# A perceiver layer's cross attention: the values' bias laid into PSUM by ACT, and outputs accumulated by ACT and POOL

## The chip, the cores and the metric

The kernel runs on one core of one Trainium2 chip. A core has a matrix engine (PE, with its weight loads shown apart as PEld), a vector engine (DVE), an activation engine (ACT), a general engine (POOL) and a queue that starts transfers (SP). Matrix products land in PSUM, a small memory of eight banks; DVE and ACT read and write PSUM, POOL here works on SBUF alone. The metric is device time in microseconds; each engine works through its own queue in order, and engines wait for each other by semaphores.

## The reference, cut to what matters

A layer of a perceiver in float32: cross attention of 128 queries per batch over a context of 2048 rows, then self attention, then a gated attention block. Batch 4, width 512, 16 heads of 32. The change lies in the cross attention alone:

```python
q = (layernorm(x) @ Wq + bq).reshape(4, 128, 16, 32)
k = (ctx @ Wk + bk).reshape(4, 2048, 16, 32)
v = (ctx @ Wv + bv).reshape(4, 2048, 16, 32)
scores = einsum('bqhd,bkhd->hbqk', q, k) / sqrt(32)
attn = softmax(scores over the 64 pairs of head and batch)   # not over the keys
out = einsum('hbqk,bkhd->bqhd', attn, v)
x = x + out @ Wo + bo
```

The softmax runs over the 64 (head, batch) pairs at one (key, query) position. So a block of keys can be finished by itself: no maximum or sum is carried from block to block, and the outputs of the blocks are simply added.

## The kernel before, in words

The context is cut into 16 blocks `n` of 128 keys (`NK` = 16, all four batches in one tile `ct`), and each block's heads into four chunks `c` of four heads. One pass of the inner loop over (`n`, `c`), called a step here, works on several blocks at once, in an order written out by hand (`manual_schedule`: every engine gets its instructions in the order of the program text). In a step of the steady part:

- `keys`: PE projects the next chunk of keys into a PSUM bank (L232), ACT copies it out with its bias (`kT`, L282).
- `values(n-1, c)`: PE projects the values of block `n-1` for batch `c` into a bank (L239), ACT copies them to `v` (L288), and POOL adds the bias row `bv_row` to `v` (L289).
- `shifted`, `exponentials_of`, `total` for block `n-1`: DVE subtracts the maximum (L342), ACT takes exponentials (L351), POOL adds up the sums (L355 to L358, and L331, L333 at the block's end).
- `attend(*done)`: PE multiplies the finished weights `sg` of block `n-2` and `v` into the bank `pso` (L386). `done` is the chunk that was scaled one step earlier.
- `scores(n, c)`: PE makes the scores in four banks (L299); ACT copies them to `sg` in two halves (L312).
- `scaled(n-2, c)`: DVE multiplies by the inverse sums (L342 again, the same helper).
- `accumulate(*done)`: DVE adds `pso` onto `acc` in SBUF (L399; for block 0 it copies, L397).
- `largest(n, c)`: DVE takes the maximum over the four banks of scores (L321, and L319 at `c` = 0); at the next block's start `largest_tail` folds it (L336).

The pools set who waits for whom: keys and values share two banks in turn (`s12_ps`, 2 buffers), the scores have four, and `pso` is a single bank (`s1_ps_o`, 1 buffer), so an `attend` waits until the one before has been read out of it. The pool `tmp` has four tiles of 128x512 under the tag `xn`.

After the loop comes a written-out ending. It attends the last scaled chunk (13, 3), shifts and exponentiates block 15, projects the rest of its values, starts the output projection with an identity product (L519), adds up the last sums on PE in `ps_sum` (L525, whose last part waits for POOL's `half_total`, L366), and then alternates `scaled`, `attend`, `accumulate` and the output projection (L546).

## Time and profile before

| | |
|---|---|
| Time, median of 3 runs | 832.28 us (831.68 to 833.19) |
| Profiled execution, its own time | 832.41 us |
| Profiled execution, span | 830.6 us |
| Granted PE clock, mean | 0.999 |
| PE busy | 813.8 us (98%) |
| DVE busy | 629.7 us (76%) |
| ACT busy | 424.4 us (51%) |
| POOL busy | 438.1 us (53%) |
| Cross attention loop and its ending | to about 644 us of the span |

Busy times are sums over one execution; L with a number is a line of the kernel. In the timeline each row is: start in us, length in us, engine, line, operation, output<-inputs, sizes, how many instructions are merged (x), and in brackets how long the engine had been idle just before and what released it. Ends of matrix products are modelled, so their starts are the firmer number.

### The profile page before, as it was taken

How to read it: one execution, taken by the hardware profiler on the slowest of the kernel's cores; microseconds unless marked ns; L12 is line 12 of the kernel's file. 1: busy time of each engine (PE TensorE's matmuls, PEld its weight loads, DVE VectorE, ACT ScalarE, POOL GpSimd, SP SyncE). 2: the span in 40 equal slices, each digit the busy share in tenths (PEclk: the TensorE clock that was granted, in tenths of full speed). 3: DMA queues.
4: the chain of work that ended last, by engine and by line, in shares of the span. 5: the costliest groups of instructions: out<-in, count | busy, mean ns of one | idle time of the engine just before them, and what ended most of it. 6: DMA issues, size and time to landing. Idle time of an engine off the chain costs nothing. (4 is left out here: it accounts for less than half of the span.)

```text
span 830.6 us, 16415 instructions
## 1 busy us (share of the span) xinstructions
PE 813.8 (98%) x7089; PEld 442.7 (53%) x7089; DVE 629.7 (76%) x636; ACT 424.4 (51%) x689; POOL 438.1 (53%) x290
## 2 busy tenths in 40 slices
PE   9999999999999999999999999999989999999998
PEld 5444455555555555555545555555544558684574
DVE  2139689889888988988898898979896488947472
ACT  2357555555555555455545654555440435934661
POOL 1244776765666576666667575666760004512251
PEclk9999999999999999999999999999999999999999
DMA  8140010101101010101101010100110132102001
GB/s 313 31 155 1 1 52 2 51 1 51 36 17 52 1 52 1 51 8 47 51 1 52 1 51 2 52 2 6 48 51 1 51 102 105 36 18 86 19 1 52
DMA packets 11418, 35.54 MB, mean 43 GB/s; under 512 B 1121, under 2 KB 1522, under 8 KB 9298
## 3 DMA queue, kind: packets, MB, share of 16 engines
q1 hardware_dynamic: 9122, 30.36, 10.6%
q10 hardware_dynamic: 1776, 3.28, 1.1%
q8 instruction: 55, 0.90, 0.4%
q0 software_dynamic: 448, 0.87, 0.4%
q14 instruction: 17, 0.14, 0.1%
HBM read 33.45 MB, written 1.05 MB: 42 GB/s over the span
## 5 line engine op out<-in xcount | busy, mean ns | idle before, releaser
L342 DVE TENSOR_TENSOR sg<-sg,stat 128x2048 f32<-128x2048 f32 x128 | 288.2, 2281 | 1.2
L239 PE MATMUL ps_v<-w_xattn_Wv,ct 128*128 128x512 f32 x512 | 230.1, 593 | 0.0
L232 PE MATMUL ps_k<-ct,w_xattn_Wk 128*128 128x512 f32 x480 | 221.9, 605 | 0.8 <-ACT pos L142 0.8
L321 DVE TENSOR_TENSOR mx<-mx,ps_s 128x1024 f32<-128x1024 f32 x96 | 117.2, 1221 | 75.7 <-ACT sg L312 63.5
L239 PEld LDWEIGHTS ps_v<-w_xattn_Wv,ct 128*128 128x128 f32 x512 | 96.9, 190 | 121.4 <-issue 117.8
L289 POOL TENSOR_TENSOR v<-v,row_xattn_bv 128x512 f32<-128x512 f32 x64 | 81.7, 1277 | 144.9 <-ACT v L288 144.9
L351 ACT ACTIVATE sg<-sg 128x2048 f32<-128x2048 f32 x64 | 122.5, 1914 | 32.0 <-DVE sg L342 32.0
L232 PEld LDWEIGHTS ps_k<-ct,w_xattn_Wk 128*128 128x128 f32 x480 | 86.2, 189 | 94.1 <-issue 86.1
L357 POOL TENSOR_TENSOR sm<-sm,sg 128x1024 f32<-128x1024 f32 x46 | 108.5, 2359 | 35.9 <-ACT sg L351 33.7
L312 ACT COPY sg<-ps_s 128x1024 f32<-128x1024 f32 x128 | 123.4, 1013 | 7.2 <-DVE mx L319 3.5
L288 ACT COPY v<-ps_v 128x512 f32<-128x512 f32 x64 | 37.6, 587 | 157.3 <-PE ps_v L239 157.3
L358 POOL TENSOR_TENSOR sm<-sm,sg 128x1024 f32<-128x1024 f32 x46 | 108.8, 2365 | 3.6
L282 ACT ACTIVATE kT<-ps_k,bk 128x512 f32<-128x512 f32 x64 | 43.9, 689 | 66.3 <-PE ps_k L232 60.4
L299 PE MATMUL ps_s<-qT,kT 32*128 32x128 f32 x2048 | 75.7, 283 | 0.1
L386 PEld LDWEIGHTS pso<-sg,v 128*32 128x32 f32 x1920 | 48.8, 109 | 46.0 <-DVE sg L342 20.9
L299 PEld LDWEIGHTS ps_s<-qT,kT 32*128 32x128 f32 x2048 | 63.3, 186 | 18.0 <-issue 17.0
L386 PE MATMUL pso<-sg,v 128*32 128x128 f32 x1920 | 64.6, 276 | 2.2 <-DVE sg L342 1.6
L355 POOL TENSOR_TENSOR sm<-sg 128x1024 f32<-128x1024 f32 x16 | 37.9, 2370 | 37.3 <-ACT sg L351 37.3
L680 POOL TENSOR_TENSOR lg<-lg,pos 128x512 f32<-128x512 f32 x6 | 7.4, 1291 | 72.9 <-ACT lg L679 72.9
L399 DVE TENSOR_TENSOR acc<-pso,acc 128x512 f32<-128x512 f32 x54 | 36.9, 683 | 3.9 <-PE pso L386 3.9
L319 DVE TENSOR_TENSOR mx<-sg,ps_s 128x1024 f32<-128x1024 f32 x16 | 19.4, 1212 | 22.8 <-ACT sg L312 22.8
L1049 POOL TENSOR_TENSOR e<-e,rs 128x512 f32<-128x512 f32 x16 | 16.3, 1041 | 36.8 <-DVE rs L1048 36.8
(224 smaller groups left out, 821.4 us busy)
## 6 DMA issues: line engine op xcount, KB each, us to landing
ct<-in_ctxT SPq DMA_DIRECT2D x15, 1024.0 KB, 5.0
ev_win<-in_tabv SPq DMA_DIRECT2D x1, 2048.0 KB, 7.2
w_xattn_Wk<-in_xattn_Wk ACTq DMA_DIRECT2D x4, 256.0 KB, 7.9
ct<-in_ctxT SPq DMA_DIRECT2D x4, 256.0 KB, 6.4
x<-in_x SPq DMA_DIRECT2D x4, 256.0 KB, 7.7
w_xattn_Wv<-in_xattn_Wv ACTq DMA_DIRECT2D x1, 1024.0 KB
w_xattn_Wq<-in_xattn_Wq SPq DMA_DIRECT2D x1, 1024.0 KB, 10.1
w_xattn_Wo<-in_xattn_Wo ACTq DMA_DIRECT2D x1, 1024.0 KB, 5.0
```

The costliest lines, as they stand in the source:

```text
L232: nc.tensor.matmul(ps, lhsT=w[:, k, c * P : (c + 1) * P], rhs=src[:, k, :], start=(k == 0), stop=(k == C - 1))
L239: nc.tensor.matmul(ps, lhsT=src[:, k, b * T : (b + 1) * T], rhs=w[:, k, :], start=(k == 0), stop=(k == C - 1))
L282: nc.scalar.activation(kT[n, c], ps, AF.Identity, bias=bk[:, c : c + 1])
L289: nc.gpsimd.tensor_tensor(v[n, b], v[n, b], bv_row, ALU.add)
L299: nc.tensor.matmul(ps[i][:, cols], lhsT=kT[n, c][rows, cols], rhs=qT[rows, c, cols], start=True, stop=True)
L312: nc.scalar.copy(sg[n, c][:, k * HALF : (k + 1) * HALF], pss[n, c][k])
L321: nc.vector.tensor_tensor(mxs[n], mxs[n], pss[n, c][k], ALU.max)
L342: nc.vector.tensor_tensor(g, g, stat[:, row, :].unsqueeze(1).to_broadcast([P, NH * B, T]), op)
L351: nc.scalar.activation(sg[n, c], sg[n, c], AF.Exp, scale=SCALE)
L357: eng.tensor_tensor(t, t, g[:, 0:HALF], ALU.add)
L358: eng.tensor_tensor(t, t, g[:, HALF:], ALU.add)
L386: nc.tensor.matmul(ps[i * HD : (i + 1) * HD, b * T : (b + 1) * T], lhsT=v[n, b][:, h * HD : (h + 1) * HD], rhs=sg[n, c][:, f * T : (f + 1) ...
```

## The change

Two parts, both in the cross attention.

The first: after the values (`n`, `b`) of blocks 1 to 14 are copied out of their bank, ACT copies `bv_row` from SBUF into the bank that the next values will use (`bias_first`), and those values' four products all add onto it (`start` is false for the first of them). The POOL addition to `v` is left out for these. The values of block 0, of block 15 and (1, 0) keep it. That is 55 of the 64.

The second: `accumulate` for block 0 is an ACT copy instead of a DVE copy. For blocks 1 to 13, without the last chunk (13, 3), ACT copies `pso` to a tile `o` in SBUF and POOL adds `o` onto `acc`; that is 51 chunks. From (13, 3) on, DVE accumulates as before.

```diff
+        def bias_first(n, b):
+            biased[n, b] = bank(f"v{n}_{b}")
+            nc.scalar.copy(biased[n, b], bv_row)
+
         def values(n, b):
             v[n, b] = vp.tile([P, D], F32, tag="v", name=f"v{n}_{b}")
-            ps = bank(f"v{n}_{b}")
-            project(ps, wv, cts[n], b)
+            ahead = (n, b) in biased
+            ps = biased[n, b] if ahead else bank(f"v{n}_{b}")
+            for k in range(C):
+                nc.tensor.matmul(
+                    ps,
+                    lhsT=cts[n][:, k, b * T : (b + 1) * T],
+                    rhs=wv[:, k, :],
+                    start=(k == 0 and not ahead),
+                    stop=(k == C - 1),
+                    skip_group_check=ahead,
+                )
             nc.scalar.copy(v[n, b], ps)
-            nc.gpsimd.tensor_tensor(v[n, b], v[n, b], bv_row, ALU.add)
+            if not ahead:
+                nc.gpsimd.tensor_tensor(v[n, b], v[n, b], bv_row, ALU.add)
+            if 0 < n < NK - 1 and (n, b) != (NK - 2, B - 1):
+                bias_first(*((n, b + 1) if b + 1 < B else (n + 1, 0)))
...
         def accumulate(n, c):
             if n == 0:
-                nc.vector.tensor_copy(acc[:, c, :], pso[n, c])
+                nc.scalar.copy(acc[:, c, :], pso[n, c])
+            elif n < NK - 2 and (n, c) != (NK - 3, C - 1):
+                o = tmp.tile([P, B * T], F32, tag="xn", name=f"o{n}_{c}")
+                nc.scalar.copy(o, pso[n, c])
+                nc.gpsimd.tensor_tensor(acc[:, c, :], o, acc[:, c, :], ALU.add)
             else:
                 nc.vector.tensor_tensor(acc[:, c, :], pso[n, c], acc[:, c, :], ALU.add)
```

In the order that the program text gives, an ACT step becomes: `kT` copy, `v` copy, bias copy, exponential, two score copies, `o` copy. In the changed kernel's numbering the bias copy is L289, the `v` copy L304, the `o` copy L420 (block 0: L417), POOL's addition L421 and the remaining DVE addition L423.

More of the change, by code (lines that the diff above doesn't have):

```diff
@@ L282, in keys_out @@
             nc.scalar.activation(kT[n, c], ps, AF.Identity, bias=bk[:, c : c + 1])
+        biased = {}
+        def bias_first(n, b):
+            biased[n, b] = bank(f"v{n}_{b}")
+            nc.scalar.copy(biased[n, b], bv_row)
         def values(n, b):
             v[n, b] = vp.tile([P, D], F32, tag="v", name=f"v{n}_{b}")
-            ps = bank(f"v{n}_{b}")
-            project(ps, wv, cts[n], b)
+            ahead = (n, b) in biased
[9 more added lines that the diff above has]
+                )
             nc.scalar.copy(v[n, b], ps)
-            nc.gpsimd.tensor_tensor(v[n, b], v[n, b], bv_row, ALU.add)
+            if not ahead:
+                nc.gpsimd.tensor_tensor(v[n, b], v[n, b], bv_row, ALU.add)
+            if 0 < n < NK - 1 and (n, b) != (NK - 2, B - 1):
+                bias_first(*((n, b + 1) if b + 1 < B else (n + 1, 0)))
         def scores(n, c):
```

## The prediction

> **What bounds the kernel now.** I read the page's busy shares first, then the busy times by stretch, then the timeline of single steps, then the waits.

> ```profile
> PE 813.8 (98%) x7089; PEld 442.7 (53%) x7089; DVE 629.7 (76%) x636; ACT 424.4 (51%) x689; POOL 438.1 (53%) x290
> ```

> A share of 98% alone proves little, as ends on PE are modelled. The stretches sharpen it (columns: length, then PE, PEld, DVE, ACT, POOL busy, granted clock, DMA share, GB/s):

> ```profile
> 420.00:460.00 40.00, 40.00 (x328) 20.52 (x329) 34.78 (x24) 23.00 (x23) 25.43 (x15) 1.00 0.09 28
> 600.00:640.00 40.00, 35.83 (x319) 17.48 (x318) 32.88 (x21) 10.23 (x9) 15.21 (x10) 1.00 0.08 27
> ```

> In the loop PE has no gap, and DVE, the engine that the change relieves, is busy 34.78 of 40. In the ending PE has gaps. One step of the loop, on PE, ACT and DVE:

> ```profile
> 574.39 1.92 ACT L351 ACTIVATE sg<-sg 128x2048 f32<-128x2048 f32 x1
> ...
> 574.81 1.17 PE L299 MATMUL ps_s<-qT,kT 32*128 32x128 f32 x32
> 575.91 3.70 PE L232 MATMUL ps_k<-ct,w_xattn_Wk 128*128 128x512 f32 x8
> 576.08 0.68 DVE L399 TENSOR_TENSOR acc<-pso,acc 128x512 f32<-128x512 f32 x1
> 576.20 1.92 ACT L312 COPY sg<-ps_s 128x1024 f32<-128x1024 f32 x2
> ...
> 578.15 2.55 DVE L321 TENSOR_TENSOR mx<-mx,ps_s 128x1024 f32<-128x1024 f32 x2 [1.40 <-ACT sg L312]
> ...
> 579.45 3.60 PE L239 MATMUL ps_v<-w_xattn_Wv,ct 128*128 128x512 f32 x8
> ...
> 579.71 0.69 ACT L282 ACTIVATE kT<-ps_k,bk 128x512 f32<-128x512 f32 x1 [1.59 <-PE ps_k L232]
> 580.62 4.48 DVE L342 TENSOR_TENSOR sg<-sg,stat 128x2048 f32<-128x2048 f32 x2
> 582.98 1.08 PE L386 MATMUL pso<-sg,v 128*32 128x128 f32 x32
> 583.08 0.59 ACT L288 COPY v<-ps_v 128x512 f32<-128x512 f32 x1 [2.69 <-PE ps_v L239]
> 583.57 1.92 ACT L351 ACTIVATE sg<-sg 128x2048 f32<-128x2048 f32 x1
> ```

> The next scores start at 583.99, so a step is 583.99 - 574.81 = 9.18 us. From 106.71 to 583.99 the starts of scores stand 477.28 / 52 = 9.18 us apart, the same at every step, and the waits view of PE from 140 to 580 us lists nothing. That includes the first step of each block, where DVE does some 3 us more (L336, 1.95; L373, 0.96). An engine whose pace is not touched by 3 us more on another is not waiting for it. So the loop is PE's, and DVE's time there is covered.

> **The change in the loop.** Counts from the two built orders: DVE loses 55 instructions, ACT gains 110, POOL loses 55 and gains 51.

> - DVE: 55 x 0.68 (L399) = 37.4 us go, all beside PE: worth 0 to PE's pace.
> - POOL: 55 additions to `v` at 1.28 go, 51 to `acc` come; the nearest row is the same form, 1.28. POOL's busy time changes by 4 x 1.28 = -5 us of 438: 0.
> - PE: as many products as before, of the same shapes.
> - ACT: 55 copies out of `pso`: the `v` copy is the same form, 0.59. The 55 bias copies (SBUF to PSUM) are no row of this trace. Bounds: 0.49, the start-to-start of the `v` copy and the exponential behind it (583.08 to 583.57), and 1.01, a 128x1024 copy (L312 by its group's mean); I take 0.59, the same size. A step of ACT is now 0.59 + 1.92 + 1.92 + 0.69 = 5.12 us and becomes 6.30 of 9.18: room, unless order makes a wait.

> So order decides, and I go through each PE wait.

> 1. Keys. The bias needs the bank that the keys had, so the keys now go to the bank that the values have just left, and wait for the `v` copy. That ended at 574.49 (573.90 + 0.59) for keys that start at 575.91: 1.42 to spare, at each step, for ACT is idle 2.69 before that copy and still about 1.5 after the `o` copy and a later `kT`.
> 2. Values wait for the bias copy: over by about 575.1 (at the dear bound 575.5), needed at 579.45.
> 3. Scores wait for `kT` and the maximum. `kT` moves behind the `o` copy: score copies end at 578.12, or 578.6 with the bias copy's 0.49 ahead of the exponential, `o` to 579.2, so `kT` keeps its place; at a block's first step (score copies end 570.46) it moves to about 572.1, needed at 574.81. The maximum moves by 0.49, from 580.70 to 581.2, needed at 583.99.
> 4. `attend` waits for the `o` copy instead of L399: 579.2, needed at 582.98.

> Does the 0.49 add up from step to step? The ring is maximum, shift, exponential, score copies, maximum; while it was behind PE, in block 2, it ran 8.59 per step (L342 at 97.41, 106.00, 114.60) and 35.27 per block, against PE's 4 x 9.18 = 36.71. The bias copy stands before the exponential, while ACT would wait for the shift anyhow; it shifts the ring once and doesn't lengthen it. At the dear bound the shift is 1.0 instead of 0.49, still inside items 1 to 4. Sum in the loop: 0.

> Queued waits: behind the `o` copy on ACT stands `kT` (item 3). POOL's addition waits for the `o` copy, with the next sums behind it; these sums wait for the next exponential, some 5 us later. No transfer moves; SP's queue is as before.

> **The change at the loop's end.** Here one wait does show:

> ```profile
> 594.19 0.68 DVE L399 TENSOR_TENSOR acc<-pso,acc 128x512 f32<-128x512 f32 x1
> 594.56 1.92 ACT L312 COPY sg<-ps_s 128x1024 f32<-128x1024 f32 x2
> ...
> 594.93 1.08 PE L386 MATMUL pso<-sg,v 128*32 128x128 f32 x32 [0.59 <-DVE acc L399]
> ```

> In the last step no keys stand between the scores and the next `attend` (13, 3), which waits until (13, 2) has left `pso`. That was DVE's addition, done at 594.87. Now it is ACT's copy, queued behind the score copies that end at 596.48: 596.48 + 0.59 = 597.07, and 0.05 more, 597.12. So `attend` (13, 3), and behind it on PE 24 products of values, the identity products and the sums, come 2.2 us later. Where do they meet the end?

> ```profile
> 610.41 1.99 PE L525 MATMUL ps_sum<-sg,ident 128*128 128x512 f32 x4 [0.47 <-ACT sg L351]
> ...
> 612.70 3.70 PE L525 MATMUL ps_sum<-sg,ident 128*128 128x512 f32 x8 [0.30 <-ACT sg L351]
> ...
> 615.07 2.35 POOL L366 TENSOR_TENSOR sm<-sm,sg 128x1024 f32<-128x1024 f32 x1
> 617.48 1.98 PE L525 MATMUL ps_sum<-sm,ident 128*128 128x512 f32 x4 [1.08 <-POOL sm L366]
> ```

> PE's idle time there is 0.47 + 0.30 + 1.08 = 1.85 by modelled ends. By starts, a product of this size takes 0.43 in a row ((612.70 - 606.34) holds 12 of them, 5.15, and 1.1 of gaps): the last eight of 612.70 could end at 616.2, so the gaps are 0.64 + 0.46 + 1.25 = 2.35. So of 2.2 us between nothing and 0.35 is left at 617.48, where POOL's L366 is late anyway. POOL's own row to 617.42 doesn't move: the addition of (13, 2) falls at 602.3, after the sums of block 14, into an idle stretch of 1.98 us before L355 at 605.51. DVE's chain starts with the maximum at 596.51, behind the same score copies. I take +0.1, between 0 and 0.35, plus at most 0.2 if the bias copy of the last steps moves the exponential.

> The sum: 832.41 for the profiled execution + 0 + 0.1 = 832.5; against the median, 0.13 lower, 832.4. What a measurement of this kernel can tell from no change is about 0.2%, or 1.7 us.

> [...] The clock is 1.00 in every stretch, and PE's longest idle stretches are 1.42 (623.64) and 1.33 us (747.3); the change makes one of 2.7 (594.4 to 597.1). What such a stretch does to the clock, no row here shows; the rows' bounds are nothing, and half speed over all 20 us up to 617, +10.
> [...]

> **The rivals.**

> - Slower, at the loop's end: the 2.2 us of `attend` (13, 3) are not covered. The point is 2.35 us: what goes beyond it, by a longer `o` copy or a slower PE behind the idle stretch, goes into the time one for one. Price for the whole wait uncovered: 832.4 + 2.1 = 834.5. For: the cover is thin, 0 to 0.2 us over. Against: POOL's L366 stands 1.08 us behind PE today.
> - Slower, on PE: another wait kind at a block's boundary costs PE a fixed piece. Starts of different products stand 0.09 to 0.2 us wider than of equal ones; 0.09 x 55 = 5 us, 837.4. Against: the first step of a block already has an extra wait instruction and POOL waits at its `attend`, and takes the same 9.18.
> - Faster: DVE paces the loop after all, or shared memory access does. All of DVE's 37.4 us would make 795; one thirtieth of it, 1.2 us, is not to be told from none. Against: equal steps, empty waits view. Or the ending gains 1 to 2 us from a DVE that is idle earlier: 831; against, its maximum at 596.51 waits for ACT.

> **How the numbers follow.** No change within 0.2%: 0.64 (its own range 831.4 to 833.6). Wait uncovered at the end: 0.18. PE boundaries and the like: 0.09. Faster: 0.09. The range 831.2 to 835.0 takes in the first two, 0.82.

> **What would show it.** Right: steps still 9.18 us apart; DVE some 37 us less busy, ACT some 60 more; one new PE wait of about 2.7 us before L406 near 594, by ACT's L420; `ps_sum`'s last part still released by POOL near 617.5. Wrong: steps of another length, a PE wait in the loop for ACT's L304 or L289, a clock below 1.00 after 597, or `ps_sum` released late by PE itself.

## The result and the profile after

The changed kernel takes 842.86 us, the median of 4 runs (841.08 to 843.08), against 831.98 for the kernel before beside it: a ratio of 1.0121, 95% interval 1.0108 to 1.0134. It is 10.9 us slower. The forecast was 832.4 with a range up to 835.0: wrong. The profiled execution of after took 841.08 us, with a span of 839.3. Of all executions below, two stand apart by a granted clock of 0.84 and 0.85 (one of e9 at 948.64 us, one of the kernel before at 935.85) and are left out of the ratios.

From the page of after, the busy shares and the clock in 40 slices of 21 us:

```profile
PE 822.0 (98%) x7089; PEld 451.3 (54%) x7089; DVE 597.8 (71%) x581; ACT 477.6 (57%) x799; POOL 431.1 (51%) x286
...
PEclk9999999999999999999999999999999996999999
```

DVE is 31.9 us less busy and ACT 53.2 more: the direction that the edit says, and less than the 37 and 60 of the prediction, for the most part since rows of one engine overlap (the `v` copy of 583.08 lasts 0.59, the row behind it starts at 583.57) and busy time counts the overlap once. The new thing is the 6 in the clock's row. The loop itself runs as before, as the same stretch of it shows (PE full, DVE down from 34.78, ACT up from 23.00), and two steps on PE and ACT from the timeline:

```profile
420.00:460.00 40.00, 40.00 (x329) 20.53 (x328) 32.41 (x19) 26.89 (x31) 25.30 (x16) 1.00 0.08 27
```

```profile
565.28 1.17 PE L319 MATMUL ps_s<-qT,kT 32*128 32x128 f32 x32
...
570.45 0.60 ACT L420 COPY o<-pso 128x512 f32<-128x512 f32 x1
...
570.93 0.71 ACT L282 ACTIVATE kT<-ps_k,bk 128x512 f32<-128x512 f32 x1
...
574.04 0.60 ACT L289 COPY ps_v<-row_xattn_bv 128x512 f32<-128x512 f32 x1
...
574.46 1.17 PE L319 MATMUL ps_s<-qT,kT 32*128 32x128 f32 x32
```

Scores still start 574.46 - 565.28 = 9.18 us apart; the new copies fit between. The costs lie behind the loop. PE's waits from 575 to 710 us (total, count, longest):

```profile
PE pso L406 <- ACT o L420: 2.7, 1, 2.7
PE pso L406 <- DVE sg L362: 1.4, 1, 1.4
...
PE s_rk L668 <- issue: 0.8, 1, 0.8
```

The first is the wait that the prediction named, at `attend` (13, 3). The last is a pause of PE with no wait on any engine, in the position products of the self attention (L668, `by_position`: 32x64 products, many small instructions), which the change doesn't touch. Before, the longest there was:

```profile
PE ps_lg L644 <- issue: 0.3, 1, 0.3
```

Now the stretches around both places, after (length; PE, PEld, DVE, ACT, POOL busy; granted clock; DMA share; GB/s):

```profile
590.00:610.00 20.00, 17.33 (x127) 8.96 (x126) 18.11 (x11) 10.80 (x10) 17.32 (x13) 0.91 0.00 1
675.00:710.00 35.00, 34.19 (x585) 29.27 (x583) 22.24 (x48) 12.54 (x25) 7.54 (x6) 0.76 0.25 92
```

Before, both stretches have clock 1.00; the second:

```profile
675.00:710.00 35.00, 34.61 (x679) 27.30 (x678) 30.09 (x65) 21.00 (x67) 11.54 (x10) 1.00 0.26 93
```

The trace's clock record has two drops to 0.5 in after: 596.37 to 599.78 (3.41 us) and 688.52 to 705.59 (17.07 us). What each did, by the starts of products:

- Loop's end: PE is idle 2.67 us and then runs at half clock for 3.41. `ps_sum` is done at 620.00 instead of 619.46, though the loop had begun 0.35 earlier: about 0.9 us. Its rows stood with three gaps before; from after's timeline, `attend` (13, 3) and `ps_sum`:

```profile
596.66 1.94 PE L406 MATMUL pso<-sg,v 128*32 128x128 f32 x32 [2.67 <-ACT o L420]
...
612.97 5.31 PE L549 MATMUL ps_sum<-sg,ident 128*128 128x512 f32 x12
618.12 1.88 PE L549 MATMUL ps_sum<-sm,ident 128*128 128x512 f32 x4
```

  PE no longer waits for POOL there: the cover is used up.
- Position products: 15.9 us before (679.42 to 695.28), 22.7 after (679.96 to 702.69), and another 2.9 us at half clock behind them. From there on everything is 8.8 us later than before.

The profiled execution is the fastest of the four. Its granted clock is 0.987, for six windows of 3.41 us at half clock; the other three have 0.985, which is about one window more (3.41 us at half clock are 0.002 of the span). No trace shows where that one fell.

So the question is why the clock drops in code that the change leaves alone.

### The profile page after: what moved, and what is told of

Its sections match the earlier page's. It is cut to its first block, busy times and chain, and to the rows that moved or that the text cites. A ratio compares the mean times of both kernels' runs of the same rounds, so it can differ in the third digit from the quotient of the medians.

```text
span 839.3 us, 16355 instructions
## 1 busy us (share of the span) xinstructions
PE 822.0 (98%) x7089; PEld 451.3 (54%) x7089; DVE 597.8 (71%) x581; ACT 477.6 (57%) x799; POOL 431.1 (51%) x286
## 4 chain that ended last, share of the span: by engine, by line
PE 89%; ACT 5%; DVE 4%; POOL 1%; issue 1%; DMA 0%; DVEq 0%; POOLq 0%; ACTq 0%
PE ps_k L232 26%; PE ps_v L296 26%; PE ps_s L319 8%; PE pso L406 7%; PE ps_q L232 3%; ACT lg L792 2%; PE s_y L1176 2%; PE s_k L232 2%; PE ps_k L436 2%; PE s_lg L668 2%; DVE sg L362 1%; PE s_v L239 1%; PE ev L863 1%; PE ps_out L570 1%; PE s_q L995 1%; PE ps_sum L549 1%
## 5 line engine op out<-in xcount | busy, mean ns | idle before, releaser
L232 PE MATMUL ps_k<-ct,w_xattn_Wk 128*128 128x512 f32 x480 | 221.9, 605 | 0.8 <-ACT pos L142 0.8
L232 PEld LDWEIGHTS ps_k<-ct,w_xattn_Wk 128*128 128x128 f32 x480 | 86.2, 189 | 94.1 <-issue 86.1
L304 ACT COPY v<-ps_v 128x512 f32<-128x512 f32 x64 | 37.5, 586 | 152.3 <-PE ps_v L296 152.3
L406 PEld LDWEIGHTS pso<-sg,v 128*32 128x32 f32 x1920 | 49.4, 110 | 48.1 <-issue 42.5
L406 PE MATMUL pso<-sg,v 128*32 128x128 f32 x1920 | 65.5, 278 | 4.3 <-ACT o L420 2.7
L421 POOL TENSOR_TENSOR acc<-o,acc 128x512 f32<-128x512 f32 x51 | 65.0, 1275 | 0.0
L282 ACT ACTIVATE kT<-ps_k,bk 128x512 f32<-128x512 f32 x64 | 44.2, 693 | 26.4 <-PE ps_k L232 22.1
L289 ACT COPY ps_v<-row_xattn_bv 128x512 f32<-128x512 f32 x55 | 32.8, 596 | 0.0
```

The source lines that it names most:

```text
L232: nc.tensor.matmul(ps, lhsT=w[:, k, c * P : (c + 1) * P], rhs=src[:, k, :], start=(k == 0), stop=(k == C - 1))
L282: nc.scalar.activation(kT[n, c], ps, AF.Identity, bias=bk[:, c : c + 1])
L406: nc.tensor.matmul(ps[i * HD : (i + 1) * HD, b * T : (b + 1) * T], lhsT=v[n, b][:, h * HD : (h + 1) * HD], rhs=sg[n, c][:, f * T : (f + 1) ...
L421: nc.gpsimd.tensor_tensor(acc[:, c, :], o, acc[:, c, :], ALU.add)
```

## The experiments

Theory A: the change adds PE instructions, which shifts PE's code so that a code fetch falls badly in the position products. Ahead of those products PE has 10,755 instructions in the trace of before and 10,798 in that of after: as many products, but 93 event instructions (waits that stand in the queue as instructions of their own) instead of 50; all 43 more stand at `attend` (L406, 57 instead of 14 at L386). Theory B: the second drop follows from the wait or the first drop. Theory C: the phase of the clock's windows (drops and rises of the clock lie on a grid of 3.41 us) against the program alone decides. Theory D, formed after the first four runs: A, but the fetch is late because of a load.

**e1: no wait at the loop's end.**

```diff
-            elif n < NK - 2 and (n, c) != (NK - 3, C - 1):
+            elif n < NK - 3 or (n == NK - 3 and c < C - 2):
```

> The changed kernel, but the accumulation of (13, 2) stays on VectorE as it was, so that attend (13, 3) does not wait behind ScalarE's score copies: the 2.67 us wait of PE at the loop's end goes, and with it the half-clock window behind it. PE's code is one instruction shorter than in the changed kernel (92 event instructions ahead of the position products instead of 93; 50 in the kernel before). Theory A (the second clock drop, 17.07 us of half clock in the position products, comes from where a PE code fetch falls: the 42 or 43 added PE instructions shift it): the wait is gone, the second drop stays, 840.5 to 842. Theory B (the second drop follows from the first one, or from the wait): both gone, 831.5 to 833. Theory C (the second drop depends on when the section starts against the clock's 3.41 us windows): anything between, differing from execution to execution.

Measured: 841.58 us, ratio 1.0104 (1.0089 to 1.0119). The same two stretches of e1:

```profile
590.00:610.00 20.00, 18.90 (x133) 9.26 (x132) 18.60 (x12) 11.33 (x10) 16.37 (x12) 1.00 0.10 35
675.00:710.00 35.00, 34.12 (x593) 29.56 (x591) 22.23 (x47) 13.67 (x31) 7.45 (x6) 0.76 0.25 92
```

The first drop is gone with its wait, the second is unchanged. Theory B falls. At the medians of four executions each the wait is worth 1.3 us; the two intervals overlap.

**e2: the kernel before, its code shifted by 44 instructions** (an fp32 product is four PE instructions here: the 256 products of the values, 64 times four, are 512 MATMUL and 512 LDWEIGHTS rows on L239 of before).

```diff
-        idle(ps, 12)
+        idle(ps, 23)
```

> The kernel before, with 23 instead of 12 warming products on PE at its very start (44 PE instructions more, where the change adds 43 before the position products); nothing else. PE's idle time at the start hides their 1 to 2 us in part. Theory A (place of the code fetch): a PE stall of about 1.0 us with no wait in the position products (0.57 us in the kernel before), 17 us of half clock behind it, 839.5 to 842. Theory B (consequence of the wait at the loop's end): no drop, 832 to 833.5. Theory C (phase of the clock windows): no fixed answer, since only the start moves.

Measured: 845.51 us, ratio 1.0151 (1.0136 to 1.0166). PE's waits and the second stretch of e2:

```profile
PE s_rk L644 <- issue: 0.7, 1, 0.7
```

```profile
675.00:710.00 35.00, 34.21 (x576) 29.59 (x574) 20.84 (x46) 12.11 (x23) 7.50 (x6) 0.71 0.20 69
```

Nothing of the change is in this kernel, and it shows the change's drop: the 1.00 us pause (by starts), then 20.48 us of half clock. It is above the expected range because the longer start put the position products 1.9 us later (681.33 against 679.42) and one window more was lost. This speaks for A.

**e3: the kernel before with (13, 2) alone moved to ACT and POOL.**

```diff
+            elif (n, c) == (NK - 3, C - 2):
+                o = tmp.tile([P, B * T], F32, tag="xn", name=f"o{n}_{c}")
+                nc.scalar.copy(o, pso[n, c])
+                nc.gpsimd.tensor_tensor(acc[:, c, :], o, acc[:, c, :], ALU.add)
```

> The kernel before, with only the accumulation of (13, 2) moved to ScalarE's copy and GpSimd's addition: the wait of PE before attend (13, 3) appears, 2.7 us, and PE's code grows by one instruction. Theory A: one half-clock window of 3.41 us behind the wait, no second drop, 832.5 to 834. Theory B: both drops, 840 to 843. The prediction's own sum (wait covered, no clock): 832.4.

Measured: ten executions, six of them from 833.25 to 835.74 and four from 840.26 to 843.18; median 835.32. Neither A nor B has that: A said never, B always. The profiled one, 842.61, has both drops, with a pause of 0.67 us in the position products, and a third, of one window, at 757.20. The granted clock was 0.985 to 0.989 in the four and 0.995 to 0.998 in the six. So the pause is not set by the code's place alone; that near some size the clock drops in one execution and holds in the next is the author's estimate from these ten. The kernel before does it too: 5 of its 81 executions beside the experiments took 839.9 to 841.2, at 0.987 to 0.990.

**e4: the wait filled with other products.**

```diff
-        attend(*done)
         largest_tail(n)
         values(n, 1)
+        attend(*done)
```

> The changed kernel, with the products of the values (15, 1) put ahead of attend (13, 3) on PE, so that they fill the 2.67 us wait; the same PE instructions in number (93 event instructions). Theory A: the first half-clock window goes, the second drop stays, 840.5 to 842. Theory B: both go, 831.5 to 833.

Measured: 841.73 us, ratio 1.0094 (1.0063 to 1.0125); nine executions from 840.99 to 843.42, one at 831.93. As A expected: clock 1.00 from 590 to 610, the second drop still there. The profiled execution lost one window more at 756.02, around the transposes `s_xT` of the gated block, which no edit touches.

**What the traces say of the pause.** In all of them PE pauses at instruction 11,200, counted from its first; before pauses at 11,456 also. These are 256 instructions apart, and the queue that the page calls "q8 instruction" brings packets of 16,384 bytes: 55 before and 56 after, where PE has 14,265 and 14,308 instructions. The packets start 257 PE instructions apart on the mean in before (the first at 184, the last at 14,063) and 256 in after (184 and 14,245), so a packet is taken to hold 256 of them. The boundary ahead is 10,944, also in the position products. With the times in us:

| | passes 10,944 | next code packet starts | reaches 11,200 | goes on | pause |
|---|---|---|---|---|---|
| before | 682.05 | 684.10 | 686.28 | 686.51 | 0.23 |
| after | 681.98 | 684.90 | 686.26 | 687.28 | 1.02 |
| e1 | 680.74 | 683.64 | 684.99 | 686.08 | 1.09 |
| e2 | 683.35 | 686.31 | 687.63 | 688.63 | 1.00 |
| e3 | 682.90 | 685.23 | 687.09 | 687.76 | 0.67 |

PE goes on 2.3 to 2.5 us after the packet's start, and the packet starts 2.0 to 3.0 us after the boundary. What holds it up is seen in the transfers of after from 680 to 692 us, in slices of 0.3 us:

```profile
GB/s 0 0 0 55 205 14 68 130 280 416 416 416 389 416 416 260 68 0 0 0 0 0 0 0 0 0 0 55 0 0 0 0 0 0 0 0 0 0 0 0
...
q1 hardware_dynamic: 528, 1.05, 25.3%
q8 instruction: 2, 0.03, 1.2%
...
w_ffn_WkT<-in_ffn_WkT SPq DMA_DIRECT2D x1, 1024.0 KB, 5.4
```

The load of `w_ffn_WkT`, 1 MB, takes the buffer that the self attention's key weights have left, and so starts just when the position products do (issued at 680.06, their first at 679.96; before 679.5 and 679.42). Its burst ends at 684.95, and the code packet starts at 684.90. This is theory D. The burst is tied to the section's start, the boundary to the code's length: 43 instructions more put the boundary 0.6 us earlier in the section (2.02 instead of 2.63 us after its start), while the packet, which waits for the burst, starts 0.3 us later in it (4.94 instead of 4.68). The pause grows by 0.8 us.

**e5: the load moved behind that of `ev_win`** on SP's queue: issued at 694.81 instead of 680.06. PE's instructions and their order are those of after, and `w_ffn_WqT` keeps its place ahead of `ev_win` on the queue.

```diff
         for c in range(C):
             keys(c)
...
+        fwq = load_w("ffn_WqT", nc.sync)
...
             in_=bass.AP(a["tabv"].tensor, a["tabv"].offset, [[HD, P], [1, T * HD]]),
         )
+        fwk = load_w("ffn_WkT", nc.sync)
...
-    fwq = load_w("ffn_WqT", nc.sync)
-    fwk = load_w("ffn_WkT", nc.sync)
```

> The changed kernel, with the load of the feed-forward key weights (w_ffn_WkT, 1 MB) issued behind that of ev_win on SyncE's queue, so that it no longer crosses the position products; PE's instructions are the same in number and order. Theory D (the stall is a PE code fetch held up by that load: in six traces the 16 KB code packet starts when the load's burst ends, and PE goes on 2.3 to 2.5 us after the packet's start): the packet starts some 2 us earlier, the stall of 1.0 us goes, no second clock drop; the wait at the loop's end and its window stay: 832.5 to 834. Theory A alone (only the place of the code matters, whatever the load does): stall and drop stay, 841 to 843. Theory C (phase of the clock windows alone): 833 to 843, different from execution to execution.

Measured: 832.96 us (831.32 to 833.82, 11 runs), ratio 1.0000 (0.9981 to 1.0020). The transfers of e5 from 680 to 692 us, then its two stretches:

```profile
GB/s 0 0 55 0 0 0 0 0 0 0 0 0 0 0 0 0 55 0 0 0 0 0 0 0 0 0 0 0 0 0 55 0 0 0 0 27 0 0 0 0
```

```profile
590.00:610.00 20.00, 17.33 (x130) 8.79 (x129) 18.01 (x11) 11.92 (x12) 17.60 (x13) 1.00 0.05 5
675.00:710.00 35.00, 34.78 (x688) 27.86 (x687) 30.46 (x65) 22.37 (x74) 12.63 (x11) 1.00 0.25 93
```

The single blips of 55 are code packets; the first starts at 680.80, 0.15 us after the boundary at 680.65, and 11,200 passes without a pause. The clock stays up in both stretches (one window is lost later, at 748.35, around `s_xT`). One load in another place takes away 842.86 - 832.96 = 9.9 of the 10.9 us; A alone, for which the load doesn't matter, falls, and so does C alone: eleven executions, none above 833.82. Nor is it the load by itself: in the traces of before and of e10 it stands in the same place, with shorter pauses (0.23 and 0.41), and the clock holds.

**e6: e5 and e1 together.** The edits are those two.

> Both at once: the changed kernel with (13, 2) accumulated by VectorE (no wait at the loop's end) and the load of w_ffn_WkT behind ev_win. Theory D: clock 1.00 from the start to the end, 831.0 to 832.3, as the prediction had it for the change itself, perhaps up to 0.8 below the kernel before, whose position products have stalls of 0.23 and 0.57 us. Theory A alone: 840.5 to 842. Theory C: mixed.

Measured: 831.52 us, ratio 0.9996 (0.9988 to 1.0005). Without the wait and without the late packet the change costs nothing that shows. Against e5 that is 832.96 - 831.52 = 1.4 us less. The profiles don't put this down to the wait: in that of e5 the clock holds at the wait, and the window lost at 748.35 makes the 1.5 us between the two (832.69 and 831.20). By the granted clock (0.998 or less), ten of the eleven executions of e5 lost at least one window and three of the eleven of e6; where, the other runs don't say.

**e7: the load moved in the kernel before.** The edit of e5 on the other kernel.

> The kernel before, with the load of w_ffn_WkT behind ev_win, nothing else. Theory D: the stalls of 0.23 and 0.57 us in its position products go, 831.0 to 832.2, and no execution near 840 (one of 19 of the kernel before was at 839.89). Theory A alone: as the kernel before, 832.2, with a rare one near 840. If the later load makes the feed-forward part wait, it shows here: 833 or more.

Measured: 831.68 us, ratio 0.9986 (0.9967 to 1.0005), highest 833.28. The pauses at 11,200 and 11,456 are gone (under 0.05 us each by starts). The gain, 0.4 us at the medians, is inside the interval; no execution came near 840.

**e8: the changed kernel, its code shifted back.**

```diff
-        idle(ps, 12)
+        idle(ps, 1)
```

> The changed kernel, with 1 instead of 12 warming products on PE at its start: 44 PE instructions less, so that the code of the position products lies as in the kernel before (one instruction earlier). The load stays where it was. Theories A and D: the boundary of the code packet comes some 0.7 us later in the section, the stall falls from 1.0 to 0.2 to 0.6 us, and the second drop goes in most executions; the wait at the loop's end and its window stay, and fewer warming products may make the start up to 2 us shorter or cost a clock window there: 830.5 to 834.5. Theory C: mixed, 832 to 843.

Measured: 835.72 us, ratio 1.0042 (1.0016 to 1.0068); eleven executions from 833.62 to 836.41, one at 844.76. In the profiled execution the second drop is gone as expected, with a pause of 0.43 us; the one at 844.76 (granted clock 0.985) fits with it. The time is above what was expected. In the profiled execution, 836.1, the clock rises at 10.7 us instead of 5.9, with one warming product; at the loop's end two windows fall instead of one; and the position products start 3.4 us later than in after.

**e9 and e10: each part of the change alone.** e9 keeps the accumulation, e10 the bias.

```diff
 e9
-            if 0 < n < NK - 1 and (n, b) != (NK - 2, B - 1):
+            if False:
 e10
-                nc.scalar.copy(acc[:, c, :], pso[n, c])
-            elif n < NK - 2 and (n, c) != (NK - 3, C - 1):
-                o = tmp.tile([P, B * T], F32, tag="xn", name=f"o{n}_{c}")
-                nc.scalar.copy(o, pso[n, c])
-                nc.gpsimd.tensor_tensor(acc[:, c, :], o, acc[:, c, :], ALU.add)
+                nc.vector.tensor_copy(acc[:, c, :], pso[n, c])
```

> The changed kernel without the bias laid first: the values' bias is added by GpSimd as before, only the accumulation goes through ScalarE and GpSimd. PE's code has 94 event instructions ahead of the position products (93 in the changed kernel, 50 before), and the wait at the loop's end is there. Theory D: the accumulation alone carries the loss: stall of 1.0 us, both drops, 841 to 843.5. If the bias copies were what costs: 832 to 833.5.

> The changed kernel with the accumulation on VectorE as before: only the bias laid first into PSUM. PE's code has 38 event instructions ahead of the position products, 12 fewer than before, and no wait at the loop's end. Theory D: the boundary of the code packet comes 0.2 us later in the section than in the kernel before, the stall at it is 0.3 us or less, no drop: 831 to 832.8. If the bias copies cost: 834 or more.

Measured: e9 843.56 us (five executions), ratio 1.0131 (1.0107 to 1.0154); e10 832.41 us, ratio 1.0003 (0.9994 to 1.0011). The accumulation carries the whole loss. Of the two drops expected for e9, its profiled execution (839.46, the fastest) has the second alone: the wait of 2.67 us is there, and the clock holds. The 12 event instructions that the bias saves move the boundary the other way, to 2.8 us after the section's start instead of 2.63; yet the pause in e10 was 0.41 us instead of the 0.3 or less expected, for the packet started 2.26 us after the boundary instead of 2.05.

**e11: the kernel before with both the shift of e2 and the load of e5.**

> The kernel before with both: 23 warming products at the start (44 PE instructions more, alone 845.5 us) and the load of w_ffn_WkT behind ev_win. Theory D: the code lies as badly as in the run with the shift alone, but the code packet no longer waits for the load: no stall, no drop, 832.1 plus the 1.9 us by which the longer start put the position products later: 833 to 835. Theory A alone: 843 to 846.

Measured: 833.57 us, ratio 1.0017 (0.9994 to 1.0040), against 845.51 with the shift alone. The second stretch of e11:

```profile
675.00:710.00 35.00, 34.80 (x662) 26.95 (x664) 30.14 (x65) 19.72 (x60) 11.07 (x10) 1.00 0.25 93
```

Shift and load are both needed for the drop; this pair shows it without any line of the change.

**e12: the changed kernel with the edits of e4 and e5**, the form that the runs point to.

> The changed kernel with the products of the values (15, 1) ahead of attend (13, 3), which fill the wait at the loop's end, and the load of w_ffn_WkT behind ev_win: what the runs point to as its best form. Theory D: clock 1.00 throughout, 830.8 to 832.2; faster than the kernel before with the same load move (831.7) only if the gaps at the end of the loop shrink by the reorder. Theory A alone: 840.5 to 842.

Measured: 831.37 us (831.05 to 832.95), ratio 0.9993 (0.9984 to 1.0002), clock 1.00 in both stretches. It is not to be told from e7 or from the kernel before. In the 55 executions of e5, e6, e7, e11 and e12, the kernels with the load moved, none is above 836.06.

## Why the prediction was wrong, point by point

- **The loop: right.** Steps of 9.18 us, PE without a gap, no wait for the bias copies or for `o`. The bias copy took 0.596 (L289) and the `o` copy 0.606 (L420), against 0.59 taken for both. e10 (1.0003), and e6 against e7, which both have the load moved (831.52 and 831.68), show the loop's price as nothing, within 0.1%.
- **The wait at the loop's end: right in place and size, and its cover too, while the clock holds.** 2.67 us idle against 2.7. From the start of the loop's last scores to that of the position products it is 86.26 us before (593.16 to 679.42), 86.22 in e5 with the wait (592.40 to 678.62). In e5, whose profiled execution has the wait and no drop there, the gaps at `ps_sum` are used up to a remainder, still released by POOL, as was written:

```profile
PE pso L406 <- ACT o L420: 2.7, 1, 2.7
...
PE ps_sum L549 <- POOL sm L386: 0.3, 1, 0.3
```

- **The clock behind that wait: the wrong end was taken.** Between nothing and half speed, the forecast took nothing for a 2.7 us stretch. In after it cost a window of 3.41 us at half clock, 1.7 us, which ate the cover: the wait for POOL at `ps_sum` is gone there, since PE is late itself. The term was +0.1 and measures 0.9 in after's profiled execution (87.14 us from 592.82 to 679.96 where before has 86.26) and nothing in e5's, where the clock held; between medians it is 1.3 (after less e1) and 1.4 (e5 less e6), not all of it shown to be the wait's. The rival "uncovered", +2.1, names the same wait at more than it measures. One reading there is off: the last stretch before, 760 to 831, reads 0.99 and not 1.00, for a drop to 0.5 at 829.15, at the very end.
- **"PE: as many products as before, of the same shapes": this step failed, and with it 9.9 us.** It counted products, not instructions. In before, DVE both scales `sg` and empties `pso`, so one wait on DVE serves `attend`; afterwards the two come from DVE and ACT, and 57 `attend`s instead of 14 have an event instruction of their own. Those instructions cost the loop nothing (steps of 9.18 us in both), so looking for their time there found none. They move all PE code behind them by 43 places against its code packets.
- **"No transfer moves": true of the order, and not enough.** The transfer that mattered stays where it was; what moved is the need for a code packet against it. The view that showed this place before was in reach: a PE wait on "issue" of 0.3 us in L644, and a packet queue by name on the page.
- **The signs.** Of those named for "wrong", two came: a clock below 1.00 after 597, and `ps_sum` released late by PE itself.

Left open: why in e3, one instruction longer than before, the packet started 2.3 us after the boundary instead of 2.05. One trace of each doesn't tell a cause from the spread of the load's own time. Why the packet waits for the load is not shown, only that it does; nor why, in before, the packet after it was late as well (started at 688.15, 1.87 us behind the boundary at 11,200, with the burst long over at 684.31), which made the pause at 11,456. The split of the 9.9 us is also only partly followed: 22.7 - 15.4 = 7.3 us in the position products (15.4 in e5) and half of the 2.9 us at half clock behind them make 8.8, in the profiled executions. And medians mix windows lost elsewhere: 20 of the 81 executions of the kernel before have a granted clock of 0.997 or 0.998, about one window lost, and take 832.85 to 833.95 us.

## What to carry to other kernels

Count what a change adds to an engine's code, event instructions included: where that engine runs through many short instructions, ask which load is in flight when it crosses a code packet's boundary, and keep large loads out of such a section (here 842.86 us with a load of 1 MB in it, 832.96 with that load behind it). A pause that a trace calls "issue" is worth following even at 0.3 us, when it stands in a section of sparse products. And a wait of PE that is covered by later gaps is covered only if the clock stays up (here 0.9 us came through in after, where it fell, and none in e5, where it held); filling it with independent products (e4, e12: clock 1.00 there) is safer than trusting the cover.
